# Two graph layers on one core: new places for statistics, weight sums, exponentials and adds in the first and last groups

## The chip, the cores and the metric

The kernel runs on one core of one Trainium2 chip. A core has five engines that run side by side, each with its own queue of instructions: TensorE (PE, with PEld for its weight loads), VectorE (DVE), ScalarE (ACT), GpSimd (POOL) and SyncE (SP). DMA transfers are started from the queues of SP, ACT and POOL. The metric is device time in microseconds (us) of one execution; the kernel before takes 2524.23 us (median of 3 runs, 2522.88 to 2525.54).

## The reference

There are 128 graphs of 128 nodes with 512 features, in fp32, and one 128 x 128 adjacency matrix. Two layers follow each other:

```python
# --- layer 0 ---
h = relu(layernorm(x))
q, k, v = h @ Wq.T, h @ Wk.T, h @ Wv.T
rel = adj.T * (q @ k.T)                    # per graph, 128 x 128
rel = rel / norm(rel, axis=2)
x = x + rel @ v
# --- layer 1 ---
h = relu(layernorm(x))
q, k, v = h @ Wq + bq, h @ Wk + bk, h @ Wv + bv     # 8 heads of 64
scores = q @ k.T / sqrt(64) + where(adj == 0, -1e9, 0)
x = x + softmax(scores) @ v
```

## The kernel before, in words

**Groups.** Four graphs make a group (`G = 4`), so there are 32 groups. A group is a `Layer0` object while it is in layer 0 and a `Layer1` object in layer 1. In the order strings below, `f` is the group that is being fetched and normalized for layer 0, `m` the group whose layer 0 is computed, `n` the same group as it enters layer 1, `l` the group whose layer 1 is computed, `p` the one whose layer 1 is being finished. `w` is an object with the steps that prepare the weights of layer 1.

**Order by hand.** All five engines run under a manual schedule: each engine executes its instructions in the order in which the program emits them. The order strings `FIRST`, `SECOND`, `ORDER` and `LAST` are lists of steps, and `run` calls the step methods from left to right. `FIRST` serves the first group, `SECOND` the second, `ORDER` all others, `LAST` the end. So a step's place in a string fixes its place in every queue that it uses, and an instruction that has to wait holds up everything behind it on its engine. Before `FIRST` there is a prologue: the statistics and transposition of group 0, the first loads, and the weights of layer 0.

**Products.** A 512 x 512 x 512 product is a `Product` object made of seven products of half size (`P1` to `P7`). `wc[n]` holds the weights' quarters and four sums of them, made by `sums` with four adds of 128 x 512: T1, T2, T3, T4N, in this order. `P1`, `P2` and `P3` use plain quarters (W11, W21, W22); `P5`, `P6`, `P7` and `P4` use T1, T2, T3 and T4N. On the other side stand quarters of the transposed activations and the sums `s[0]` to `s[3]`, which `sumA` (s0, s1) and `sumB` (s3, s2) make on DVE. A product keeps its results in three PSUM banks, x, y and z; the pool `ps_mm` has four banks. `P1` starts bank x and ACT copies it out (`r1`); `P2` starts y and DVE adds `r1` to it; `P5` starts z, copied by ACT (`r5`); `P6` goes on in x, copied (`r2`); `P3` goes on in z, and DVE adds `r2`; `P7` goes on in x, and DVE adds `r5`; `P4` goes on in x and ACT copies it. The copies lie in the pool `rpool`, four buffers used in turn. `G`, `V` belong to layer 0; `Q`, `K`, `V` to layer 1 (with biases).

**Other steps.**
- `stat(b)`: two DVE instructions per graph, L283 and L284. `inv(i)`: four small POOL instructions for two graphs, L290 to L293, giving `rstd` and `shift`.
- `hn(i)`: two ACT instructions (L301) normalize two graphs; ACT then sends them to DRAM (`d_h`, L184). `rd(i)`: four DMAs on SP (L192) fetch them in another arrangement (`u_h`). `T(i)`: DVE transposes 32 x 32 blocks (L313) into `h`. In the prologue `hn_pe` and `turn_pe` do the same through TensorE (L335).
- `weights0` multiplies Wq and Wk of layer 0 into one matrix on TensorE (`pa`, L123), DVE copies the four results out (`place`, L114 and L115) and makes the sums of `a`. `weights_v0` transposes Wv on TensorE (`pwv`, L139, PSUM banks of the same pool as `pa`), ACT copies it out, and POOL makes the sums `v0` from the buffer `v12` of `rpool`.
- `load1` issues the weights of layer 1 as DMAs from POOL's queue. `w.scale` is three ACT multiplies on the weights of q; `w.sumq`, `w.sumk` are sums on DVE, `w.sumv` on POOL.
- `R`, `mask_rel`, `square`, `N`, `norms`, `O`, `xO`: layer 0's 128 x 128 products on TensorE (L382), mask on DVE (L391), squares on ACT (L398), their sums on TensorE (L408), the root `rn` on DVE and POOL (L417, L418), the output product (L422), and the residual add on DVE (L428).
- `S`, `mk`, `ex`, `wr`, `wt`, `A`, `oc`, `rdo`, `ot`: layer 1's scores on TensorE (L453, one set of PSUM banks: `S1` waits until `ex0` has read the scores of graph 0), mask and maximum on DVE, exponentials on ACT (L471), their way through DRAM (`d_w`, `u_w`) and DVE's transposition, the output product (L570), its copy by ACT (L581), the way back (`d_o`, `u_o`), the division by the sums on DVE (L598), and POOL's residual add (L605).
- In `LAST` the last two graphs go another way: `mkA`, `mkB`, `exA`, `exB`, `tw` (L519), `An` (L530), and `fin(b)`, which divides on DVE (L539), adds to x on POOL or DVE (L547) and sends the result from SP (L548).

`load(g, b, queue)` starts the load of one graph's x (L70). `xpool` has twelve buffers, so three groups fit. The method `Layer.load` issues one only if the graph isn't loaded or being loaded yet.

Of the kernel before, what the change touches and what calls it, by code (L numbers as in the profile page):

```python
# [11 lines left out]
ALU = mybir.AluOpType  # L12
# [3 lines left out]
G = 4  # L16
# [5 lines left out]
def kernel(  # L22
# [15 lines left out]
    nc = tc.nc  # L38
# [29 lines left out]
    def load(g: int, b: int, queue):  # L68
        xb = xpool.tile([P, D], F32, tag="xb", name=f"xb_{g}_{b}")
        queue.dma_start(xb, x[g * G + b])  # L70
        x_tiles[g, b] = xb
# [16 lines left out]
    def sums(n: str, w12, eng):  # L88
        c = wc[n]
        eng.tensor_tensor(c[:, T1], w12, c[:, W11], ALU.subtract)  # L90
        eng.tensor_tensor(c[:, T2], c[:, W22], c[:, T1], ALU.subtract)
        eng.tensor_tensor(c[:, T3], c[:, W22], w12, ALU.subtract)
        eng.tensor_tensor(c[:, T4N], c[:, W21], c[:, T2], ALU.subtract)
# [16 lines left out]
    w12 = {}  # L110

    def place(n: str, m: int, ps, w12, copy):

        copy(wc[n][:, W11 if m < 2 else W21, m % 2, :], ps[:, 0:HF])  # L114
        copy(w12[:, m, :] if m < 2 else wc[n][:, W22, m % 2, :], ps[:, HF:D])  # L115

    def weights0(between):

        a12 = rpool.tile([P, 2, HF], F32, tag="r", name="a12")
        pa = [ps_mm.tile([P, D], F32, tag="mm", name=f"pa_{m}") for m in range(KD)]  # L120
        for k in range(KD):
            for m in range(KD):
                nc.tensor.matmul(  # L123
                    pa[m], lhsT=raw["q"][:, k, ts(m, P)], rhs=raw["k"][:, k, :],
                    start=(k == 0), stop=(k == KD - 1),
                )
            if k == KD - 2:
                between()
        for m in range(KD):
            place("a", m, pa[m], a12, nc.vector.tensor_copy)  # L130
        sums("a", a12, nc.vector)

    def weights_v0():

        v12 = rpool.tile([P, 2, HF], F32, tag="r", name="v12")
        for m in range(KD):
            pt = ps_mm.tile([P, KD, P], F32, tag="mm", name=f"pwv_{m}")
            for k in range(KD):
                nc.tensor.transpose(pt[:, k, :], raw["v"][:, k, ts(m, P)], ident)  # L139
            place("v0", m, pt.rearrange("p k e -> p (k e)"), v12, nc.scalar.copy)  # L140
        sums("v0", v12, nc.gpsimd)
        nc.vector.tensor_scalar(mask, adj_sb, 0.0, NEG, ALU.is_equal, ALU.mult)

    def load1():
        for name, w in (("q", wq1), ("k", wk1), ("v1", wv1)):
            wr = w.rearrange("(k p) d -> p k d", p=P)
            nc.gpsimd.dma_start(
                wc[name][:, W11 : W21 + 1].rearrange("p h k d -> p (h k) d"), wr[:, :, 0:HF]
            )
            nc.gpsimd.dma_start(wc[name][:, W22], wr[:, 2:4, HF:D])  # L150
            w12[name] = wpool.tile([P, 2, HF], F32, tag="wT", name=f"w12_{name}")
            nc.gpsimd.dma_start(w12[name], wr[:, 0:2, HF:D])
        nc.gpsimd.dma_start(bq_sb, bq1.rearrange("(e p) -> p e", p=P))
        nc.gpsimd.dma_start(bk_sb, bk1.rearrange("(e p) -> p e", p=P))
        nc.gpsimd.dma_start(bv_sb, bv1.partition_broadcast(P))

    class Weights1:
        def scale(self):

            SC = HD**-0.5  # L160
            nc.scalar.mul(wc["q"][:, 0:3], wc["q"][:, 0:3], SC)
            nc.scalar.mul(w12["q"], w12["q"], SC)
            nc.scalar.mul(bq_sb, bq_sb, SC)

        def sumq(self):
            sums("q", w12["q"], nc.vector)
# [199 lines left out]
    class Layer0(Layer):  # L366
        n = 0
# [62 lines left out]
    class Layer1(Layer):  # L430
        n = 1
# [104 lines left out]
        def fin(self, b):  # L536
            g, xb = self.g, x_tiles.pop((self.g, b))
            o = work.tile([P, D], F32, tag="o", name=f"o_{g}_{b}")
            nc.vector.tensor_tensor(  # L539
                o.rearrange("p (k r d) -> p k r d", k=NH, r=2),  # L540
                self.po.pop(b).rearrange("p (k r d) -> p k r d", k=NH, r=2),
                self.rs.pop(b).rearrange("p (r k) -> p k r", r=2)[:, :, :, None].to_broadcast(
                    [P, NH, 2, HD]
                ),
                ALU.mult,
            )
            (nc.vector if b == G - 1 else nc.gpsimd).tensor_tensor(xb, xb, o, ALU.add)  # L547
            nc.sync.dma_start(out[g * G + b], xb)  # L548

        def mkA(self, b):  # L550
# [58 lines left out]


    FIRST = """
        m.sumA m.sumB m.start m.G.P1 f.hn0 f.rd0 m.G.P2 m.G.P5 w.scale m.G.P6 w.sumq m.G.P3 m.V.P1 f.hn1 f.rd1
        w.sumv m.G.P7 m.V.P2 w.sumk m.G.P4 m.V.P5
        m.R m.mask_rel m.square f.T0 m.V.P6 m.V.P3 m.N m.norms m.V.P7 m.O0 m.xO0 m.O1 m.xO1 n.stat0 n.stat1
        n.inv0 m.V.P4 n.hn0 n.rd0 f.T1 m.O2 m.O3 f.sumA f.start f.G.P1 m.xO2 m.xO3 n.stat2 n.stat3 n.inv1
        f.G.P2 f.sumB f.G.P5 n.hn1 n.rd1 f.G.P6 f.G.P3 f.G.P7 n.T0 f.G.P4 n.T1 n.start
    """.split()
    SECOND = """
        l.Q.P1 l.sumA l.Q.P2 l.sumB l.K.P1 l.K.P2 l.Q.P5 l.Q.P6 f.load0 f.load1 l.Q.P3 l.K.P5 l.K.P6 l.Q.P7
# [16 lines left out]
    """.split()  # L636
    LAST = """
        l.Q.P1 p.rdo0 l.sumA l.Q.P2 l.sumB l.K.P1 l.K.P2 p.wt3 l.Q.P5 p.ot0 l.Q.P6 l.Q.P3 l.K.P5 l.K.P6 l.K.P3
        l.Q.P7 l.S0 l.mk0 l.K.P7 l.Q.P4 l.ex0 l.wr0 l.K.P4 l.S1 l.mk1 p.A1 p.oc1 p.rdo1 l.start_v l.V.P1
        l.ex1 l.V.P2 l.V.P5 l.S2 l.mkA2 l.mkB2 l.V.P6 l.exA2 l.exB2 l.wt0 l.wr1 l.V.P3 l.V.P7 l.S3 l.mkA3 l.mkB3  # L640
        l.tw2 l.wt1 l.exA3 l.exB3 l.V.P4 l.An0 l.fin0 l.An1 l.fin1 p.ot1 l.tw3 l.An2 l.fin2 l.An3 l.fin3
    """.split()
# [1 line left out]
    def run(order, **who):  # L644
        for step in order:
            name, *path = step.split(".")
            at = who.get(name)
            if at is None:
                continue
            if len(path) == 2:  # L650
                getattr(getattr(at, path[0]), path[1])()
            elif path[0][-1].isdigit():
                getattr(at, path[0][:-1])(int(path[0][-1]))
            else:
                getattr(at, path[0])()

    with tc.manual_schedule(engines={EN.PE, EN.SP, EN.Pool, EN.DVE, EN.Activation}):
        p, l, m = None, None, Layer0(0)
        for b in range(G):
            m.stat(b)  # L660
        m.inv(0)
        m.inv(1)
        for b in range(G):
            load(1, b, nc.gpsimd)
        load1()
        m.hn_pe(0)
        m.hn_pe(1)
        f = Layer0(1)
        for b in range(G):
            f.stat(b)  # L670
        f.inv(0)
        f.inv(1)
        weights0(lambda: m.turn_pe(0))
        m.turn_pe(1)
        weights_v0()
        for g in range(NG):
            n = Layer1(g)
            if g:
                f = Layer0(g + 1) if g + 1 < NG else None
            run((FIRST, SECOND, ORDER)[min(g, 2)], p=p, l=l, m=m, n=n, f=f, w=Weights1())  # L680
            p, l, m = l, n, f
        run(LAST, p=p, l=l)
# [30 lines left out]
```

## Time and profile before

| | us |
|---|---|
| median of 3 runs | 2524.23 |
| lowest, highest | 2522.88, 2525.54 |
| the profiled execution, its own time | 2526.15 |
| its span in the trace | 2524.4 |
| TensorE busy in the span | 2497.9 (99%) |
| DVE busy | 1709.2 (68%) |
| ACT busy | 1022.3 (40%) |
| POOL busy | 534.7 (21%) |

The profile is of one execution, whose own time is 1.92 us above the median; about 1.75 us of it lie outside the span. A line of the timeline reads: start, length, engine, line of the code, operation, output <- inputs, shapes, and in brackets the idle time of the engine before it with what ended it. "PE" rows of eight matmuls with L218 are one half-size product. POOL's times are rough, and TensorE's ends are modelled.

### The profile page before, as it was taken

What the parts mean: (1) busy time and instruction counts of PE and PEld (TensorE: products, weight loads), DVE (VectorE), ACT (ScalarE), POOL (GpSimd) and SP (SyncE); (2) the same over time, 40 slices, a digit from 0 to 9 for tenths busy, and PEclk for the clock granted to TensorE, in tenths of its full rate; (3) what the DMA queues carried; (4) which work ended last, traced back from release to release, by engine and by line L of the source; (5) the groups of instructions that cost most, each with busy time, mean ns of one, the idle gap of its engine ahead of it and who ended that gap; (6) DMA issues with size and microseconds to landing.
All of it is one profiled execution on the core that took longest, in us unless ns stands there. A gap on an engine that the chain in (4) does not pass through costs nothing.

```text
span 2524.4 us, 40790 instructions
## 1 busy us (share of the span) xinstructions
PE 2497.9 (99%) x14672; PEld 2106.7 (83%) x14672; DVE 1709.2 (68%) x2484; ACT 1022.3 (40%) x3248; POOL 534.7 (21%) x945
## 2 busy tenths in 40 slices
PE   8999999999999999999999999999999999999998
PEld 6788888888888888888888888888888888888886
DVE  5566766676776667666767766676667676666766
ACT  3344443444433444344444434443444444344433
POOL 4121222112122212221121222122211212221211
PEclk9999999999999999999999999999999999999999
DMA  5255554556445555445564455554455644555543
GB/s 172 84 176 175 166 156 141 182 161 199 147 145 159 176 175 167 152 147 176 160 197 146 144 165 173 178 167 152 147 175 162 197 148 143 164 176 176 167 135 101
DMA packets 370475, 405.71 MB, mean 161 GB/s; under 512 B 29600, under 2 KB 286752, under 8 KB 370272
## 3 DMA queue, kind: packets, MB, share of 16 engines
q1 hardware_dynamic: 278992, 167.92, 25.2%
q10 hardware_dynamic: 70384, 166.74, 18.4%
q0 software_dynamic: 20896, 68.44, 8.2%
q8 instruction: 115, 1.88, 0.3%
q14 instruction: 88, 0.72, 0.1%
HBM read 204.80 MB, written 198.18 MB: 160 GB/s over the span
## 4 chain that ended last, share of the span: by engine, by line
PE 97%; DVE 1%; DMA 1%; ACT 0%; issue 0%; POOL 0%; SPq 0%; ACTq 0%; DVEq 0%; POOLq 0%
PE pv_x L218 18%; PE pq_x L218 9%; PE pv_z L218 9%; PE pk_x L218 9%; PE pg_x L218 9%; PE pss L453 6%; PE po L570 5%; PE pv_y L218 5%; PE pg_z L218 4%; PE pq_z L218 4%; PE pr L382 4%; PE pk_z L218 4%; PE po L422 4%; PE pk_y L218 2%; PE pg_y L218 2%; PE pq_y L218 2%
## 5 line engine op out<-in xcount | busy, mean ns | idle before, releaser
L471 ACT ACTIVATE e<-pss,nmax 128x128 f32<-128x128 f32 x1008 | 354.1, 379 | 178.0 <-DVE nmax L464 156.2
L605 POOL TENSOR_TENSOR xb<-xb,o 128x512 f32<-128x512 f32 x124 | 158.3, 1276 | 1108.8 <-DVE o L598 1083.9
L218 PE MATMUL pv_x<-wc_v,h 128*128 128x256 f32 x1280 | 300.8, 382 | 0.0
L218 PEld LDWEIGHTS pv_x<-wc_v,h 128*128 128x128 f32 x1280 | 240.3, 190 | 51.0 <-DVE v L242 11.8
L301 ACT ACTIVATE hn<-xb,shift,rstd 128x512 f32<-128x512 f32 x252 | 190.9, 807 | 153.5 <-POOL shift L293 153.4
L313 DVE STREAM_TRANSPOSE h<-u_h 128x1024 f32<-128x1024 f32 x126 | 156.4, 1242 | 133.0 <-DMA u_h<-d_h 130.4
L218 PE MATMUL pv_z<-wc_v,s 128*128 128x256 f32 x1024 | 246.0, 383 | 0.0
L471 ACT ACTIVATION_READ_ACCUMULATOR e<-pss,nmax 128x1 f32 x1008 | 220.7, 219 | 0.0
L218 PEld LDWEIGHTS pv_z<-wc_v,s 128*128 128x128 f32 x1024 | 192.6, 191 | 29.2 <-DVE pv_r L235 0.4
L462 DVE TENSOR_TENSOR pss<-pss,mask 128x1024 f32<-128x1024 f32 x126 | 154.7, 1228 | 81.0 <-PE pss L453 75.5
L218 PE MATMUL pv_x<-wc_v,s 128*128 128x256 f32 x768 | 184.9, 384 | 0.0
L218 PE MATMUL pq_x<-h,wc_q 128*128 128x256 f32 x768 | 184.8, 383 | 0.0
L283 DVE BATCH_NORM_STATS2 st<-xb 128x6 f32<-128x512 f32 x256 | 172.1, 672 | 16.0 <-DMA xb<-in_x_dram 16.0
L218 PE MATMUL pk_x<-h,wc_k 128*128 128x256 f32 x768 | 181.5, 379 | 0.0
L453 PEld LDWEIGHTS pss<-kT,qT 64*128 64x128 f32 x2048 | 124.2, 187 | 54.4 <-issue 27.0
L218 PEld LDWEIGHTS pq_x<-h,wc_q 128*128 128x128 f32 x768 | 143.2, 190 | 23.8 <-ACT oT L581 5.1
L218 PEld LDWEIGHTS pk_x<-h,wc_k 128*128 128x128 f32 x768 | 145.8, 190 | 19.9
L290 POOL TENSOR_SCALAR rstd<-mv 128x2 f32<-128x2 f32 x128 | 28.9, 226 | 630.0 <-DVE mv L284 629.8
L218 PEld LDWEIGHTS pv_x<-wc_v,s 128*128 128x128 f32 x768 | 140.8, 190 | 20.5 <-issue 0.2
L464 DVE TENSOR_REDUCE nmax<-pss 128x8 f32<-128x1024 f32 x126 | 154.3, 1224 | 4.3
L486 DVE STREAM_TRANSPOSE wT<-u_w 128x1024 f32<-128x1024 f32 x126 | 150.7, 1196 | 5.2 <-DMA u_w<-d_w 5.0
L453 PE MATMUL pss<-kT,qT 64*128 64x128 f32 x2048 | 148.7, 285 | 2.6 <-ACT e L471 2.3
(147 smaller groups left out, 4416.8 us busy)
## 6 DMA issues: line engine op xcount, KB each, us to landing
d_h<-hn ACTq DMA_DIRECT2D x126, 512.0 KB, 3.6
u_h<-d_h SPq DMA_DIRECT2D x504, 128.0 KB, 3.5
d_w<-e ACTq DMA_DIRECT2D x126, 512.0 KB, 2.7
u_w<-d_w SPq DMA_DIRECT2D x504, 128.0 KB, 3.1
xb<-in_x_dram POOLq DMA_DIRECT2D x124, 256.0 KB, 3.3
d_o<-oT ACTq DMA_DIRECT2D x62, 512.0 KB, 4.3
u_o<-d_o SPq DMA_DIRECT2D x248, 128.0 KB, 3.6
out_dram<-xb POOLq DMA_DIRECT2D x124, 256.0 KB, 3.0
```

Of the source, the lines that this page charges most:

```text
L218: nc.tensor.matmul(ps[:, m, :], lhsT=lhsT, rhs=rhs, start=first and m == 0 and k == 0, stop=k == 1, skip_group_check=True,)
L283: nc.vector.bn_stats(st, x_tiles[g, b])
L301: nc.scalar.activation(hn[:, r], x_tiles[g, b].rearrange("p (k j q) -> p j k q", j=TB, q=BK), AF.Relu, bias=self.shift[:, b : b + 1], scal ...
L313: nc.vector.transpose(half.rearrange("p k (t i) -> p t k i", i=BK), self.u.pop(i).rearrange("p t (k q) -> p t k q", q=BK),)
L382: nc.tensor.matmul(pr[:, b, :], lhsT=self.turned(k, b), rhs=self.gT[:, k, ts(b, P)], start=(k == 0), stop=(k == KD - 1),)
L453: nc.tensor.matmul(pss[:, r, k, :], lhsT=self.qT[rows, k, ts(b, P)], rhs=self.kT[rows, k, ts(b, P)], start=True, stop=True,)
L462: nc.vector.tensor_tensor(sc, sc, mask[:, None, :].to_broadcast([P, H, P]), ALU.add)
L464: nc.vector.tensor_reduce(self.nmax[b], sc, AX.X, ALU.max, negate=True)
L471: nc.scalar.activation(e[:, :, i, :], sc[:, i, :].rearrange("p (j q) -> p j q", q=BK), AF.Exp, bias=nmax[:, i : i + 1], accum_out=self.tot ...
L486: nc.vector.transpose(self.wT[b].rearrange("p h (t i) -> p t h i", i=BK), self.uw.pop(b).rearrange("p t (h q) -> p t h q", q=BK),)
L570: nc.tensor.matmul(po[r * HD : (r + 1) * HD, k, :], lhsT=self.v[:, b, ts(2 * k + r, HD)], rhs=wT[:, r * NH + k, :], start=True, stop=True,)
L605: nc.gpsimd.tensor_tensor(xb, xb, o.rearrange("p k t q -> p (k t q)"), ALU.add)
```

## The change

The change alters places only; what is computed stays the same, apart from which engine does one add.

- The statistics of group 1 (`f.stat`, `f.inv`) leave the prologue, where they stood ahead of `weights0`, and go into `FIRST`, two graphs after `m.start` and two after `m.G.P2`.
- The sums of `v0` on POOL leave `weights_v0` and become the step `w.sumw` behind `f.inv1`.
- `f.hn0 f.rd0` move from behind `m.G.P1` to behind `m.G.P5`, `w.scale` from behind `m.G.P5` to behind `m.G.P6`.
- `w.sumq` moves from behind `m.G.P6` to behind `m.V.P2`; `w.sumk` moves from behind `m.V.P2` to the layer 0 products of group 1, behind `f.sumB`.
- A new step `w.loadx` issues the four loads of group 2's x from POOL's queue behind `w.sumv`. In `SECOND` the steps `f.load0` to `f.load3` then find them loaded and issue nothing.
- `m.xO2 m.xO3 n.stat2 n.stat3 n.inv1` move ahead of `f.sumA f.start f.G.P1`.
- In `LAST`, `l.ex0 l.wr0` move ahead of `l.Q.P4`.
- `fin(2)` adds on DVE, as `fin(3)` does, in place of POOL.

```diff
@@ weights_v0
             place("v0", m, pt.rearrange("p k e -> p (k e)"), v12, nc.scalar.copy)
-        sums("v0", v12, nc.gpsimd)
+        w12["v0"] = v12
         nc.vector.tensor_scalar(mask, adj_sb, 0.0, NEG, ALU.is_equal, ALU.mult)
@@ class Weights1
+        def sumw(self):
+            sums("v0", w12["v0"], nc.gpsimd)
+
+        def loadx(self):
+            for b in range(G):
+                load(2, b, nc.gpsimd)
@@ Layer1.fin
-            (nc.vector if b == G - 1 else nc.gpsimd).tensor_tensor(xb, xb, o, ALU.add)
+            (nc.vector if b >= G - 2 else nc.gpsimd).tensor_tensor(xb, xb, o, ALU.add)
@@ orders
     FIRST = """
-        m.sumA m.sumB m.start m.G.P1 f.hn0 f.rd0 m.G.P2 m.G.P5 w.scale m.G.P6 w.sumq m.G.P3 m.V.P1 f.hn1 f.rd1
-        w.sumv m.G.P7 m.V.P2 w.sumk m.G.P4 m.V.P5
+        m.sumA m.sumB m.start f.stat0 f.stat1 f.inv0 m.G.P1 m.G.P2 f.stat2 f.stat3 f.inv1 w.sumw m.G.P5 f.hn0 f.rd0 m.G.P6
+        w.scale m.G.P3 m.V.P1 f.hn1 f.rd1 w.sumv w.loadx m.G.P7 m.V.P2 w.sumq m.G.P4 m.V.P5
         m.R m.mask_rel m.square f.T0 m.V.P6 m.V.P3 m.N m.norms m.V.P7 m.O0 m.xO0 m.O1 m.xO1 n.stat0 n.stat1
-        n.inv0 m.V.P4 n.hn0 n.rd0 f.T1 m.O2 m.O3 f.sumA f.start f.G.P1 m.xO2 m.xO3 n.stat2 n.stat3 n.inv1
-        f.G.P2 f.sumB f.G.P5 n.hn1 n.rd1 f.G.P6 f.G.P3 f.G.P7 n.T0 f.G.P4 n.T1 n.start
+        n.inv0 m.V.P4 n.hn0 n.rd0 f.T1 m.O2 m.xO2 m.O3 m.xO3 n.stat2 n.stat3 n.inv1 f.sumA f.start f.G.P1
+        f.G.P2 f.sumB w.sumk f.G.P5 n.hn1 n.rd1 f.G.P6 f.G.P3 f.G.P7 n.T0 f.G.P4 n.T1 n.start
     """.split()
     LAST = """
         l.Q.P1 p.rdo0 l.sumA l.Q.P2 l.sumB l.K.P1 l.K.P2 p.wt3 l.Q.P5 p.ot0 l.Q.P6 l.Q.P3 l.K.P5 l.K.P6 l.K.P3
-        l.Q.P7 l.S0 l.mk0 l.K.P7 l.Q.P4 l.ex0 l.wr0 l.K.P4 l.S1 l.mk1 p.A1 p.oc1 p.rdo1 l.start_v l.V.P1
+        l.Q.P7 l.S0 l.mk0 l.K.P7 l.ex0 l.wr0 l.Q.P4 l.K.P4 l.S1 l.mk1 p.A1 p.oc1 p.rdo1 l.start_v l.V.P1
@@ prologue
         f = Layer0(1)
-        for b in range(G):
-            f.stat(b)
-        f.inv(0)
-        f.inv(1)
         weights0(lambda: m.turn_pe(0))
```

## The prediction

> **What bounds the kernel now.** The page first: TensorE is busy for 99% of the span, so over the middle of the run nothing can be won by moving work of other engines.
>
> ```profile
> PE 2497.9 (99%) x14672; PEld 2106.7 (83%) x14672; DVE 1709.2 (68%) x2484; ACT 1022.3 (40%) x3248; POOL 534.7 (21%) x945
> ```
>
> So I asked next for TensorE's own waits over the whole run ("waited for: us in total, times, longest"). The four longest beside the first load:
>
> ```profile
> PE pwv L139 <- issue: 3.1, 1, 3.1
> PE pg_x L218 <- DVE gT L242: 2.8, 2, 2.0
> PE pq_z L218 <- DVE qT L242: 2.6, 1, 2.6
> PE pss L453 <- ACT e L471: 2.3, 2, 2.0
> ```
>
> Then the chain of waits shows where they lie and what follows (start, length, what):
>
> ```profile
> 21.54 3.08 issue
> 24.63 3.48 PE pwv L139 x16
> ...
> 42.63 1.29 DVE gT L242 x2
> ...
> 43.96 2.92 PE pg_x L218 x8
> 46.88 2.48 PE pv_z L218 x8
> ...
> 72.18 7.40 DMA d_h<-hn
> ```
>
> Eight matmuls of L218 take 1.73 us elsewhere in this chain, eight transposes of L335 take 0.87. So the work after each of the first two stalls runs at half speed. The stretches give TensorE's granted clock behind the busy times (third number from the end):
>
> ```profile
> 22.00:24.00 2.00, 0.00 (x0) 0.00 (x0) 1.75 (x5) 0.20 (x1) 2.00 (x4) 1.00 0.99 334
> 24.00:26.00 2.00, 1.37 (x7) 1.40 (x8) 2.00 (x7) 0.25 (x1) 1.85 (x3) 0.60 1.00 350
> 46.00:48.00 2.00, 2.00 (x7) 1.55 (x6) 1.54 (x3) 0.58 (x1) 0.00 (x0) 0.50 0.30 77
> 84.00:88.00 4.00, 1.43 (x7) 0.94 (x6) 3.81 (x6) 0.05 (x1) 0.00 (x0) 1.00 0.00 0
> ```
>
> The timeline names what the stalls wait for:
>
> ```profile
> 23.80 0.39 DVE L114 COPY wc_a<-pa 128x256 f32<-128x256 f32 x1
> ...
> 40.95 1.75 DVE L93 TENSOR_TENSOR wc_q<-wc_q 128x512 f32<-128x512 f32 x1
> 42.63 0.68 DVE L242 TENSOR_TENSOR gT<-pg_z,pg_r 128x512 f32<-128x512 f32 x1
> ...
> 70.61 2.26 POOL L70 DMA_DIRECT2D xb<-in_x_dram  x4
> ```
>
> ```profile
> 2482.91 0.84 ACT L229 ACTIVATE qT<-pq_x,bq_sb 128x256 f32<-128x256 f32 x2 [7.36 <-PE pq_x L218]
> ...
> 2516.73 1.95 DVE L547 TENSOR_TENSOR xb<-xb,o 128x512 f32<-128x512 f32 x1
> ```
>
> **The change part by part.** The order of TensorE's own instructions is untouched, so I carry its timeline forward and ask, for each wait, whether the operand is there.
>
> *Statistics of the second group, out of the prologue.* DVE's copies of pa (L114) stand behind four f.stat, which wait for x of group 1 until 22.18; the copies start at 23.80 although pa_0 is complete at about 18.1. The pwv transposes need those PSUM banks. Without the stats the copies go out as pa completes, the last at 21.5; pwv starts at 21.54 without a stall: 3.08. The clock then isn't lost: 16 transposes at the 0.109 of L335 are 1.74 in place of 3.48: 1.74. Together 4.8 us. What the stats cost in their new place: DVE's block from the last pa copy to the end of sumB takes 5.3 (26.51 to 31.83), so it ends at 26.8; two stats (0.82 a pair of instructions) end at 28.5. POOL is tied up by load1's DMAs until 28.36 in both versions, so inv0 starts at 28.6 against 28.43. It took 2.86 here and 1.6 to 2.0 later in the trace; I take the slow row, 31.45. stat2, stat3 lie behind the P2 add and end at 30.8, before POOL wants them.
>
> *hn0 one product later; sums v0 named sumw.* ACT then does r5 (by 29.3), hn0 (31.45 to 33.0), r2 (to 33.65). G.P7 on TensorE, now 1.74+3.08 earlier, accumulates over the bank that r2 reads, at 33.65. That is a dead heat: between 0 and 0.5 lost, I take 0.2. POOL's sumw runs 33.3 to 38.4 (4 x 1.28), in the same place on POOL as before. Its third operation frees v12's buffer at about 37.1, which by the rotation of four may hold up V.P1's r copy on ACT, and behind it hn1 and the P4 copy (39.9 at worst); R needs that at 40.6, so the cover is 0.7.
>
> *sumq behind the V.P2 add.* In the trace four SBUF adds of 1.65 to 1.80 (POOL adds at the same time; 0.68 alone) stand before the P3, P7 and V.P2 adds, and G.P4 waits 2.02 for them. Moved back, P7's add is done 0.9 before G.P4 wants it: 2.02. Again the clock: 2.92+2.48 for G.P4 and V.P5 becomes 3.46: 1.94. Together 4.0 us, R begins at 40.6. sumq itself now runs 38.4 to 45.4 beside sumv, and mask_rel behind it ends at 46.1 instead of about 44.9; square ends at 46.8, TensorE wants it at 47.6 after V.P6 and V.P3. Those two products hide it; without them it would cost about 1.3.
>
> Here a rule speaks against me. The Trainium skill, "TensorE: Matmul & The Clock Gate", section "HAM oscillation — how this bites in real kernels", puts the limit for idle gaps at about 3.4 us; both gaps are shorter, so by it no clock is at stake and the sum is 3.7 us smaller. The granted clock of 0.50 after 2.02 idle says otherwise here, while 2.57 idle at 84.9 kept 1.00. I go by the rows.
>
> *What moves with these steps.* f.rd0 and f.rd1 are eight fetches on SP (36.12 to 45.17 before) that wait for the ACT sends behind hn0 and hn1; SP has nothing else in this phase, the first set goes out at about 36 as before, the second a little earlier, and T0 and T1 want them at 46 and 54: hidden, with 4 us or more of cover. w.scale (1.49+0.62+0.19 on ACT) now follows r2 and holds V.P1's r copy to 36.2, inside the 37.1 named above. sumk (3.2 in its old place at 44.42) is taken out of the stretch ahead of mask_rel, where nobody waited for it, so I count nothing for its going.
>
> *loadx.* Four DMA issues, 2.3 in all on POOL (row above), move from 70.6 to behind sumv, about 45.3 to 47.7, in front of rn (norms), which POOL gets at 48.8: cover 1.1, and if it is gone rn is late by the excess. SP's queue isn't reordered. The second send of n (d_h) then has no 1 MB of loads beside it: the 7.40 becomes about 3.2 (median 2.9 in that stretch, 3.2 over the first 160 us). T1 for n comes 4 us earlier; the stall of 2.57 before pq_z, and 0.2 of refilling after it (1.99 for 1.73), goes: 2.8 us. What is late next there is TensorE itself, with about 1.4 to spare. xO2, xO3 and the stats before sumA put s0 at 59.1 against a need at 59.3; sumk (4 x 0.68) ends as the P3 add becomes possible. Both taken at 0; bounds -0.3 to +0.5.
>
> *LAST, ex0 before Q.P4.* nmax is ready at 2481.8, but ACT waits for pq_x first (7.36). With ex0 first, its 2.90 end at 2484.7; K.P4 ends on TensorE at 2484.6. The stall of 1.99 before S1 becomes 0.15: 1.8 us. The copies of Q.P4 and K.P4 then end at 2486.4, before oc1 and V.P1's bank need them. wr0 brings one ACT send and four SP fetches with it; SP keeps its order (rdo0, wr0, rdo1, wr1), and wt0 wants the data only at about 2498, so the earlier fetch gains nothing and costs nothing. A gain above 2.0 is excluded, since K.P4 itself ends then; below, the bound is 1.0, if mk1 or oc1 come to wait for ACT instead.
>
> *Add of fin2 on DVE.* POOL's last add (1.27) blocks DVE's last add, 1.95 for 0.68. Now DVE adds twice: the first beside POOL's second L605 add, ending 0.55 after it (as L598 does: 1.21 and 1.25) at 2516.5, o at 2517.1, the last add at 2517.8 against 2518.68: 0.9 us. The two bounds: 0.5 and 1.3. The output DMA follows the last add as before.
>
> Sum: 4.8 + 4.0 + 2.8 + 1.8 + 0.9 - 0.2 = 14.1 us. The profiled execution took 2526.15 (span 2524.4 and 1.75 around it), so 2512.05; the median of the runs shown lies 1.92 below that execution, so 2510.1.
>
> **Rivals.** *The third stall stays or another takes its place* (22%): the send's 7.40 is not the loads' doing, or s0, r2 or rn come a little late. For: thin covers of 0.2 to 1.1. Against: typical sends of 2.9. Gain 8 to 11.5, about 2514.5. *The dead heat is lost* (9%): hn0 late on ACT delays r2, G.P7 waits 2 us, and the clock halves again as it did after 2.02 idle: with later waits the gain falls to 5 to 8, about 2518. *Too small to tell, or the order doesn't take effect as read* (3%): within 5.0 us, which is 0.2% and about what a measurement of this kernel can tell from no change. *Slower* (4%): loadx on POOL is blocked ahead of rn, since POOL's queue is in order; then O2 lacks its PSUM bank and TensorE stands. The cover is 1.1 on POOL and about 2 until O2; from a hold of 17 us beyond the issues' 2.3 the gain is gone, and from 22 us the kernel is slower by more than 0.2%. At such a hold of 30 us the time would be about 2537 (30 - 3.1 lost against 14.1). Nothing in the trace shows an issue above 0.8, all twelve buffers of xpool suffice for three groups.
>
> **How the numbers follow.** Forecast 62%, 2508 to 2512.5; rivals 22, 9, 3 and 4%. A range of 2507.5 to 2516 takes in the forecast, the first rival and the bounds above. Faster by over 0.2%: 93%; same 3%; slower 4%.
>
> **What would show it.** pwv at 21.5 with a clock of 1.00 through 20 to 50; G.P4 without a wait, R at about 40.6; d_h of n's second half landing in under 4 us and no wait of pq_z for qT; in LAST, S1 about 0.15 after K.P4; the last DVE add of 0.7. It is wrong if TensorE waits for r2 near 33, N for sq near 47, or if the middle slices fall below their present busy share.

## The result and the profile after

The changed kernel takes 2512.07 us (median of 6 runs, 2511.32 to 2513.92) against 2524.22 in the same group of runs: a ratio of 0.9953, 95% interval 0.9941 to 0.9966. A second group gave 2512.45 and 0.9947 (0.9933 to 0.9960). That is 12 to 13 us faster; 14.1 was forecast.

The profiled execution took 2513.92, its span is 2512.1. Of the four entries that stood at the top of TensorE's own waits before (waited for: total, times, longest), those of pwv and pq_z are gone, the one for gT fell from 2.8 to 0.8 and the one for e from 2.3 to 0.5. What is left at the top:

```profile
PE pa L123 <- DMA raw_q<-in_L_gnn_Wq_dram: 5.1, 1, 5.1
PE pg_x L225 <- DVE gT L249: 0.8, 1, 0.8
PE po L429 <- ACT v L233: 0.7, 1, 0.7
PE pw L526 <- DVE o L546: 0.5, 1, 0.5
PE pss L460 <- ACT e L478: 0.5, 2, 0.3
```

The chain of waits (start, length, what; the code moved down by seven lines, so L218 is L225 now) runs through the three old stalls of the first groups without a gap:

```profile
5.09 13.61 PE pa L123 x24
18.71 0.87 PE pt L342 x8
...
23.02 0.87 PE pt L342 x8
23.89 1.75 PE pwv L139 x16
25.64 1.73 PE pg_x L225 x8
...
37.72 1.73 PE pv_y L225 x8
39.45 1.73 PE pg_x L225 x8
41.18 1.73 PE pv_z L225 x8
42.90 3.57 PE pr L389 x32
...
76.63 1.73 PE pk_y L225 x8
78.36 1.73 PE pq_z L225 x8
```

The work that ran at 0.60 and 0.50 before (pwv, and G.P4 with V.P5) now lies at 23.9 to 25.6 and at 39.5 to 42.9. The granted clock, the third number from the end, is 1.00 in these stretches:

```profile
24.00:26.00 2.00, 2.00 (x18) 1.95 (x17) 1.97 (x4) 2.00 (x8) 2.00 (x3) 1.00 0.91 270
32.00:40.00 8.00, 8.00 (x39) 7.04 (x38) 2.75 (x6) 5.99 (x9) 7.41 (x12) 1.00 0.61 183
40.00:50.00 10.00, 10.00 (x67) 8.97 (x68) 8.30 (x7) 2.39 (x4) 8.07 (x8) 1.00 0.67 204
```

And the end of its chain:

```profile
2470.07 1.94 PE pk_x L225 x8
...
2475.66 1.16 PE pss L460 x16
...
2506.23 0.69 DVE xb L554
```

The two spans differ by 12.3. Cut at the same instructions in both chains, the difference is:

| block, from and to | before | after | gained | forecast |
|---|---|---|---|---|
| first pt to pg_x of G.P1 | 11.76 | 6.93 | 4.83 | 4.8 |
| to R | 21.26 | 17.26 | 4.00 | 4.0 |
| to pq_z of Q.P5 | 38.10 | 35.46 | 2.64 | 2.8 |
| to S0 of LAST | 2390.66 | 2390.62 | 0.04 | 0 |
| S0 to S1 | 8.46 | 6.68 | 1.78 | 1.8 |
| S1 to the end of the last DVE add | 32.09 | 31.26 | 0.83 | 0.9 |
| from there to the end of the span | 5.72 | 5.18 | 0.54 | not counted |
| start to the first pt | 16.35 | 18.71 | -2.36 | 0 |

The middle of the run is the same to 0.04 us in 2390. The blocks with a forecast came out, 14.1 us in sum, the end of the span gave 0.54 more, and 2.36 were lost before the first block, where the change moves nothing of TensorE's: pa's first 24 pieces began 0.8 later and took 13.61 for 12.06. The column "before" is the profile from which the forecast was made, so the agreement shows that nothing new stood in the way afterwards; it doesn't show that these stalls are typical of the kernel before. So the questions for the experiments: is that start chance, and if it is, why do the medians still differ by only 12 to 13?

### The profile page after: what moved, and what is told of

It reads as the page before. It is cut to its first block, busy times and chain, and to the rows that moved or that the text cites. A ratio compares the mean times of both kernels' runs of the same rounds, so it can differ in the third digit from the quotient of the medians.

```text
span 2512.1 us, 40787 instructions
## 1 busy us (share of the span) xinstructions
PE 2495.4 (99%) x14672; PEld 2104.9 (84%) x14672; DVE 1707.6 (68%) x2485; ACT 1023.6 (41%) x3248; POOL 532.3 (21%) x944
## 4 chain that ended last, share of the span: by engine, by line
PE 97%; DVE 1%; DMA 1%; ACT 1%; issue 0%; SPq 0%; POOL 0%; ACTq 0%; DVEq 0%
PE pv_x L225 18%; PE pq_x L225 9%; PE pg_x L225 9%; PE pv_z L225 9%; PE pk_x L225 9%; PE pss L460 5%; PE pg_z L225 5%; PE po L577 5%; PE pv_y L225 4%; PE pq_z L225 4%; PE pr L389 4%; PE pk_z L225 4%; PE po L429 4%; PE pg_y L225 2%; PE pk_y L225 2%; PE pq_y L225 2%
## 5 line engine op out<-in xcount | busy, mean ns | idle before, releaser
L225 PE MATMUL pv_x<-wc_v,h 128*128 128x256 f32 x1280 | 300.8, 382 | 0.0
L225 PEld LDWEIGHTS pv_x<-wc_v,h 128*128 128x128 f32 x1280 | 240.3, 190 | 51.0 <-DVE v L249 11.7
L225 PE MATMUL pv_z<-wc_v,s 128*128 128x256 f32 x1024 | 245.1, 382 | 0.0
L225 PEld LDWEIGHTS pv_z<-wc_v,s 128*128 128x128 f32 x1024 | 192.0, 190 | 28.6
L225 PE MATMUL pv_x<-wc_v,s 128*128 128x256 f32 x768 | 184.9, 384 | 0.0
L225 PE MATMUL pq_x<-h,wc_q 128*128 128x256 f32 x768 | 184.7, 383 | 0.0
L225 PE MATMUL pk_x<-h,wc_k 128*128 128x256 f32 x768 | 181.5, 379 | 0.0
L225 PEld LDWEIGHTS pq_x<-h,wc_q 128*128 128x128 f32 x768 | 143.3, 190 | 23.6 <-ACT oT L588 5.1
L225 PEld LDWEIGHTS pk_x<-h,wc_k 128*128 128x128 f32 x768 | 145.8, 190 | 19.9
L225 PEld LDWEIGHTS pv_x<-wc_v,s 128*128 128x128 f32 x768 | 140.8, 190 | 20.6 <-issue 0.2
```

The source lines that it names most:

```text
L225: nc.tensor.matmul(ps[:, m, :], lhsT=lhsT, rhs=rhs, start=first and m == 0 and k == 0, stop=k == 1, skip_group_check=True,)
```

## The experiments

Each kernel was timed in five rounds or more against the kernel before on the same chip. Three groups ran on three chips; ratios are against before in the same group. The changed kernel ran again in the first group only (with "hn0 behind G.P6", "Products in the first stall" and the first warm start), so "slower" below is the distance from its 2512.45 and in most cases lies between chips. The medians of before in the three groups are 2525.66, 2524.56 and 2524.38, so a distance of about 1 us isn't clear by itself; the blocks of the traces are given beside it.

**The changed kernel again.** No edit.

> The changed kernel as it is, once more, beside the others of this group. The profiled pair gave 14.6 us of gain behind the first TensorE work and 2.4 us of loss inside it (pa's first 24 pieces took 13.6 us for 12.1 and began 0.8 later), yet the timed medians differ by 12.15. Theory 1 (clock): TensorE's half-speed phases fall differently in every execution, both at the start and behind the old stalls, so the profiled 3.7 us of clock is more than the average; another profile of this kernel should show another length of pa's 24 pieces (12 to 14 us) with everything behind it shifted as a block, and R 24.2 us after the end of those pieces' first transposes, within 0.3. Theory 2 (moved wait): in executions with an earlier start the wait of G.P7 for r2 appears, since POOL's statistics hang on load1's DMAs and not on TensorE; then an early start shows a gap before G.P7 of up to 2 us. Median expected within 1.5 us of 2512.

Measured: 2512.45 (2511.83 to 2513.35), ratio 0.9947. Its chain:

```profile
4.83 12.43 PE pa L123 x24
17.26 0.87 PE pt L342 x8
...
34.55 1.73 PE pg_x L225 x8
...
41.46 3.57 PE pr L389 x32
```

R begins 24.20 us after the first pt, against 24.19 in the other profile: everything behind the start moves as one block. G.P7 (pg_x at 34.55) follows without a gap although the start was earlier, so the moved wait was not seen here. The times of this kernel spread by 2.6 us over its 11 executions in both groups, and its clock is 0.999 in all of them. The kernel before is different. Its 47 executions in the three groups, by the mean granted clock of each:

| mean clock | executions | mean us | from, to |
|---|---|---|---|
| 0.996 | 7 | 2527.99 | 2526.61, 2529.47 |
| 0.997 | 13 | 2526.07 | 2524.36, 2527.61 |
| 0.998 | 24 | 2524.29 | 2521.75, 2526.49 |
| 0.999 | 3 | 2522.34 | 2521.53, 2523.75 |

The same program spreads over 8 us, and time goes with clock: 1.9 us for each 0.001. The profiled execution of before is one at 0.997. Its three executions at the clock of the changed kernel, 0.999, still take about 10 us more than the changed kernel does: which suggests (from three executions, and a clock given to 0.001) that some 10 of the 12 to 13 us are waits and the rest goes with the clock.

**hn0 behind G.P6.**

```diff
-  ... w.sumw m.G.P5 f.hn0 f.rd0 m.G.P6
-  w.scale ...
+  ... w.sumw m.G.P5 m.G.P6 f.hn0 f.rd0
+  w.scale ...
```

> The changed kernel with f.hn0 f.rd0 one product later still, behind G.P6, so that ACT copies r2 before it waits for POOL's shift. Theory 2 (G.P7 waits for r2 in typical executions): 1 to 2.4 us faster than the changed kernel, about 2510. Theory 1 (clock): no difference, within 0.7 us of the changed kernel, since G.P7 did not wait in the profiled execution.

Measured: 2512.69 (2512.62 to 2513.97), ratio 0.9948, no difference from the changed kernel beside it on the same chip. The second theory falls as an account of the missing 2 us: r2 doesn't cost them.

**Products in the first stall of before.**

```diff
         m.turn_pe(1)
+        hot = ps_o.tile([P, D], F32, tag="po", name="hot")
+        for i in range(3):
+            nc.tensor.matmul(hot, lhsT=raw["q"][:, 0, 0:P], rhs=raw["k"][:, 0, :], start=True, stop=True)
         weights_v0()
```

> The kernel before with three products of 128x512 put on TensorE into its first stall (behind the second set of transposes, ahead of pwv; their results are not used). The stall stays, pwv still starts at about 24.6, but TensorE is busy in it. Theory 1: the clock is then full at pwv, its 16 transposes take 1.75 us in place of 3.48, and the median falls by 1.7 us times the share of executions in which the clock was halved there: 0.9 to 1.7 us below before. Rival (the slow transposes come from waiting for the banks one by one, not from the clock): pwv still takes 3.5 us and the time stays within 0.5 us of before.

Measured: 2525.34 (2522.88 to 2529.35) against 2525.66, ratio 0.9999 (0.9991 to 1.0007): no gain to be seen, and still a spread of 6.5 us. The interval reaches down to 2.3 us, so the timing alone doesn't exclude the 0.9 to 1.7 of the expectation; the chain and the granted clock behind it show why half of that can't come:

```profile
25.91 0.66 PE pwv L139 x4
26.58 0.66 PE pwv L139 x4
...
44.16 1.99 PE pg_x L218 x8
46.15 1.73 PE pv_z L218 x8
```

```profile
24.00:29.00 5.00, 4.70 (x23) 2.69 (x22) 4.62 (x12) 2.35 (x8) 3.57 (x5) 1.00 1.00 341
```

With the clock at 1.00, each four of the sixteen transposes still take 0.66: that is the pace of two L114/L115 copies of 0.33 that free one bank. Of the 1.74 that the forecast put down to the clock behind the first stall, 0.9 is this pace, and at most 0.8 the clock. (Both went, since in the changed kernel the copies run while pa still computes.) The second stall was 1.7 us long in this execution, and the products behind it ran at full speed; in the profile of before the stall of 2.0 was followed by 2.92 and 2.48. So the same gap doesn't always halve the clock.

**Parts undone, one at a time.** All from the changed kernel.

*Statistics back in the prologue.*

```diff
-  m.start f.stat0 f.stat1 f.inv0 m.G.P1 m.G.P2 f.stat2 f.stat3 f.inv1 w.sumw
+  m.start m.G.P1 m.G.P2 w.sumw
...
+        for b in range(G):
+            f.stat(b)
+        f.inv(0)
+        f.inv(1)
         weights0(lambda: m.turn_pe(0))
```

> The changed kernel with only the statistics of group 1 back in the prologue (all other parts of the change kept). The first stall must come back: DVE's copies of pa start behind the last stat, at about 23.8 to 25, and pwv waits 3 us. By the prediction's term 4.8 us slower than the changed kernel (2517). By what the run with products in the stall showed (banks are freed 0.66 apart, so pwv takes 2.64 even at full clock): 3.1 + 0.9 for sure and up to 0.8 for the clock, so 4.0 to 4.8. Rival (a stall so early is absorbed by the wait of G.P7 for r2, since hn0 hangs on POOL): 2 us or less.

Measured: 2516.27 (2515.08 to 2517.72), ratio 0.9966 (0.9954 to 0.9979); 3.8 slower than 2512.45, just under the expected 4.0 to 4.8. The stall is back in its waits and its chain, with a fallen clock behind it:

```profile
PE pwv L139 <- issue: 2.9, 1, 2.9
```

```profile
24.47 3.52 PE pwv L139 x16
```

```profile
24.00:28.00 4.00, 3.53 (x17) 3.56 (x18) 3.97 (x11) 1.94 (x6) 2.87 (x4) 0.57 1.01 327
```

In this trace the block from the first pt to G.P1 takes 11.64 (16.34 to 27.98) against 6.93: 4.7, the size of the term. The start of this execution was as quick as that of before.

*hn0 back behind G.P1.*

```diff
-  m.G.P1 m.G.P2 f.stat2 f.stat3 f.inv1 w.sumw m.G.P5 f.hn0 f.rd0 m.G.P6
+  m.G.P1 f.hn0 f.rd0 m.G.P2 f.stat2 f.stat3 f.inv1 w.sumw m.G.P5 m.G.P6
```

> The changed kernel with f.hn0 f.rd0 back behind G.P1, ahead of r5 on ACT. ACT then holds r5 until POOL's shift (about 31 to 33) and two normalizations are through, r5 ends about 33.5 to 35.5, and G.P3, which wants it at about 30.5 to 31.5, waits 3 to 4 us; with that a chance of a halved clock behind it. Expected 3 to 5.5 us slower than the changed kernel, with a wider spread of its runs. Rival (hn0's place is free, what matters are the stats alone): within 0.7 us.

Measured: 2517.06 (2515.13 to 2518.25), ratio 0.9968 (0.9956 to 0.9980); 4.6 slower, inside the expected 3 to 5.5, and with a spread of 3.1. The wait has its name, and the clock behind it (third from the end) fell:

```profile
PE pg_z L225 <- ACT pg_r L233: 4.0, 1, 4.0
```

```profile
34.00:40.00 6.00, 5.29 (x17) 4.38 (x18) 0.69 (x1) 3.07 (x5) 5.91 (x5) 0.72 0.54 176
```

From the first pt to R it takes 30.18 (16.84 to 47.02) against 24.19: 6.0 in this execution, the slowest of its six. So the move of hn0 behind P5 carries as much as that of the statistics: without it the wait goes from pwv to r5.

*sumq back ahead of P3's add.*

```diff
-  w.scale m.G.P3 ... m.V.P2 w.sumq m.G.P4
+  w.scale w.sumq m.G.P3 ... m.V.P2 m.G.P4
```

> The changed kernel with w.sumq back ahead of G.P3's add. The prediction's term: 2.0 of wait and 1.9 of clock, 4.0 slower (2516). The run with products in the first stall showed the same wait of 1.7 with full clock behind it. Theory (the clock falls only in some executions): 2.0 to 3.5 slower in the median, and a wider spread than the changed kernel's 1.5 us, with granted clocks of 0.998 among the runs. Rival (sumq's four adds end before they hurt, since POOL's sums are later now): under 1 us.

Measured: 2520.10 (2518.68 to 2522.56, 16 runs), ratio 0.9982 (0.9974 to 0.9989); 7.6 slower, more than twice the 2.0 to 3.5 that were expected. Its waits, and DVE in its timeline:

```profile
PE pg_x L225 <- DVE gT L249: 5.4, 2, 4.6
```

```profile
36.47 0.73 DVE L90 TENSOR_TENSOR wc_q<-w_q,wc_q 128x512 f32<-128x512 f32 x1 [4.07 <-ACT w_q L162]
...
40.48 1.75 DVE L93 TENSOR_TENSOR wc_q<-wc_q 128x512 f32<-128x512 f32 x1
42.15 0.68 DVE L249 TENSOR_TENSOR gT<-pg_z,pg_r 128x512 f32<-128x512 f32 x1
```

The sums can't begin before w.scale on ACT (36.47, before it was 35.85), while TensorE now comes to G.P4 about 3 us sooner; so the wait is 4.6 and no longer 2.0. Behind it G.P4 and V.P5 took 3.78 and 2.16 for 1.73 each, at a granted clock of 0.58: another 2.5, and 7.1 together. The parts aren't independent: each one removes a stall behind which the next one would grow.

*The loads of x back in SECOND.*

```diff
-  f.hn1 f.rd1 w.sumv w.loadx m.G.P7
+  f.hn1 f.rd1 w.sumv m.G.P7
```

> The changed kernel without w.loadx: the four loads of group 2's x go out in SECOND again, behind n.inv1. Prediction's term: d_h of n's second half lands after about 7 us in place of 3, pq_z waits 2.6 for qT, 2.8 slower (about 2515.2). Rival (the send is slow for itself, or T1 came late because of where the statistics stood): d_h lands in about 3, less than 0.8 slower. With a halved clock in some executions up to 1.7 more.

Measured: 2513.86 (2513.15 to 2514.94), ratio 0.9956 (0.9944 to 0.9969); 1.4 slower, half of the term and between the two expectations; by itself it is hardly clear of the distance between chips. The chain shows the mechanism as forecast, with a shorter wait (pk_y ends at 76.63 here, so 1.4 for 2.57):

```profile
63.83 6.43 DMA d_h<-hn
...
78.04 1.99 PE pq_z L225 x8
```

The send d_h is 512 KB. With the 1 MB of loads beside it, it landed in 7.40, 6.8 (in "Products in the first stall") and 6.43 us; in the eleven profiles of kernels that keep w.loadx, no send of this stretch took more than 3.3. So the rival, that the send is slow for itself, falls.

In this profile the dead heat at G.P7 was lost: its start was the earliest of those with the moved statistics (first pt at 16.66), r2 is copied to 33.95, TensorE goes on at 34.00, the product takes 1.99 in place of 1.73, and R begins 24.51 after the first pt instead of 24.20. That is the moved wait of the second theory, at 0.3 us and not 2.

*ex0 back behind Q.P4.*

```diff
-  l.K.P7 l.ex0 l.wr0 l.Q.P4 l.K.P4
+  l.K.P7 l.Q.P4 l.ex0 l.wr0 l.K.P4
```

> The changed kernel with l.ex0 l.wr0 behind l.Q.P4 again. Prediction's term: S1 waits 2.0 for the exponentials in place of 0.2, everything behind it is later by as much: 1.8 slower (about 2514.2), in some executions up to 1.7 more if the clock falls behind the wait. Rival (the end hangs on the last DVE and DMA work and has slack): under 0.6.

Measured: 2515.14 (2513.94 to 2515.71), ratio 0.9960 (0.9946 to 0.9973); 2.7 slower, inside the expected 1.8 to 3.5. The wait is there again:

```profile
PE pss L460 <- ACT e L478: 2.3, 2, 2.0
```

From S0 to S1 its chain takes 8.47 against 6.68: 1.8, the size of the term. The clock stayed at 1.00 behind it in this profile; that the rest of the 2.7 is clock in other executions is possible (two of its five runs have 0.998), but not shown. The move of fin2's add was not run by itself; its 0.83 is read from the two chains. The moves of w.sumw, w.scale, w.sumk and of xO2, xO3 with their statistics were not undone either; nothing was counted for them.

**Towards a faster version.** The start was the largest loss left, so TensorE was kept busy before its weights land. This version and the three behind it also have hn0 behind G.P6, as above.

```diff
+    hot = ps_o.tile([P, P], F32, tag="po", name="hot")
+    for i in range(8):
+        nc.tensor.matmul(hot, lhsT=ident, rhs=ident, start=True, stop=True)
...
-            if k == KD - 2:
+            if k == KD - 1:
                 between()
```

> The changed kernel with hn0 behind G.P6 as in e9, with eight products of 128x128 on TensorE from about 1.3 us on, before the first weights land (results not used), and with the first transposes of h behind all of pa. Theory 1: the clock is full sooner, pa's 24 pieces take 10.3 to 11.5 us in place of 12 to 13.6, the spread of the runs shrinks, and the median falls 1 to 3 us below the changed kernel (2509 to 2511). Rival (the slow beginning of pa is a wait for the weights' loads): pa takes as long as before, no gain; up to 0.5 us slower by the products that are added.

Measured: 2518.31 (2515.09 to 2519.39), ratio 0.9967, 5.9 slower than the changed kernel on the same chip. Outside the hand-made order the products came out behind ten pieces of pa (at 11.44 in the chain), so this run says nothing on the idea. In its trace R began at 43.95, and TensorE waited 2.1 for the squares (sq) at N of the second group. With the same lines as the first ones inside the manual schedule:

> As the run with products ahead of the first weights, but now they stand first in TensorE's order (there they came out behind ten pieces of pa, and cost time without warming anything): eight products of 128x128 from 1.4 us on; hn0 behind G.P6; the first transposes behind all of pa. Theory 1: the clock is full about 3 us sooner against pa; pa's 32 pieces take 14 to 15.5 us in place of 16 to 17, transposes in a row cost 0.6 of waiting, net 0.5 to 2 us faster than the changed kernel. Rival (the first pieces are slow because their weights land late): no gain, 0 to 1 us slower.

Measured: 2513.52 (2511.99 to 2515.35), ratio 0.9955 (0.9943 to 0.9968): no gain. Yet pa's 32 pieces took 14.37 in one go for 15.87 and 17.05 (24 and 8 together) in the two profiles of the changed kernel, and R began at 40.77. In the profiled execution, the slowest of the five (2515.35), the gain was lost later, at N of the second group:

```profile
5.13 14.37 PE pa L123 x32
...
98.49 4.86 DMA d_w<-e
...
111.95 3.54 PE pv_x L225 x8
```

The send of the weights took 4.86 where 2.6 to 2.8 is usual, DVE's mask stands behind that data, N waited 1.8 for it, and the product behind took 3.54 for 1.92, at a granted clock of 0.58. So there was an edit for this, and another for the 0.8 that G.P4 waits for P7's add:

```diff
-  f.G.P7 n.T0 f.G.P4 n.T1 n.start
+  f.G.P7 n.T0 n.T1 n.start
...
-  l.Q.P1 l.sumA ...
+  l.Q.P1 m.G.P4 l.sumA ...
...
-  l.wr1 l.wt0 m.R m.mask_rel m.square
+  l.wr1 m.R m.mask_rel l.wt0 m.square
```

> A version that should beat both: the changed kernel with hn0 behind G.P6; with group 1's G.P4 taken out of FIRST and put behind l.Q.P1 in SECOND, so that a product lies between P7 and P4 (P4 waits 0.8 for DVE's add of P7 in all traces so far); and with SECOND's m.mask_rel ahead of l.wt0, so that the mask doesn't stand behind the data from DRAM on DVE (that wait cost 1.8 us and a halved clock in two of the profiles). Theory: 1.0 to 1.5 us faster than the changed kernel (2511), with no wait for sq at about 110. Rival (the waits are met again one step later, by wt0 or by pq's banks): within 0.5 of the changed kernel.

Measured: 2514.52 (2513.54 to 2515.08), ratio 0.9958: 2 slower than the changed kernel, and outside both expectations, though the rival's reason (the wait is met again one step later) holds. Q.P1 needs T0, and T0 stands on DVE behind P7's add, which in turn waits for P7:

```profile
PE pq_x L225 <- issue: 2.0, 1, 2.0
```

```profile
69.18 2.82 PE pq_x L225 x8
72.00 2.56 PE pg_x L225 x8
```

The wait of 0.8 became 2.0, and the two products behind it took 2.82 and 2.56 for 1.73, at a granted clock of 0.57. The wait for sq is gone from its list, so the other edit did its part. Last, this version with the eight products first in TensorE's order and the transposes behind all of pa:

> The version before this one in the list, with the eight products on TensorE ahead of the first weights and the first transposes behind all of pa. In the run that had the warm start alone R began 0.7 to 2.1 us earlier than in three profiles of the kernel without it (40.8 against 41.5, 41.7 and 42.9), and the gain was lost to the wait for sq at 110. If that wait is what ate it, this version is 0.7 to 2 us faster than the other (2509 to 2510); if the early start is taken back elsewhere (r2, sumq ahead of mask_rel), no difference.

Measured: 2513.53 (2512.56 to 2514.75), ratio 0.9955: 1.0 below the run before it, at the low end of the expectation but with overlapping runs (2513.54 to 2515.08 there), and not below the changed kernel. No version of these beats the changed kernel.

## Why the prediction was right, and where its sizes were off

**Right.** The direction, the range, and the mechanism of the parts: in the table above every block came out within 0.2 of its term, and each of the four stalls came back when its part was undone (fin2's add alone was not undone). The covers held and were wider than forecast in the profile after: POOL was free 2.9 before rn (forecast 1.1), the squares were done 2.1 before N (0.8). The hold of V.P1's copy by v12 didn't show: in the second profile the copy began at 35.55, while POOL's third operation ran to 37.00. The debit of 0.2 for r2 was 0 in two profiles of the changed kernel and 0.3 in the run without loadx; in the first two a late start hid it, which is luck. Going by the rows for the clock was right too. The rule of about 3.4 us, which the prediction takes from the Trainium skill ("TensorE: Matmul & The Clock Gate", "HAM oscillation — how this bites in real kernels"), would have left no clock to win. But shorter gaps were followed by a low granted clock in further runs: 2.9 by 0.57 (statistics back), 2.0 by 0.57 and 1.8 by 0.58 (two of the versions that were meant to be faster). The gaps of 4.0 and 4.6 fit the rule. Other short gaps kept 1.00: 1.7 (products in the stall) and 2.0 (ex0 back). So no length of gap divides the two here.

**Too large.** The sum was 14.1, the medians moved by 12.15 and 13.2; the intervals of the two ratios (8.6 to 14.9 us and 10.1 to 16.9) both hold 14.1, so this shortfall alone isn't clear of noise. The forecast median of 2510.1 was clearly too low, though: the lowest of the 11 executions of the changed kernel is 2511.32. The step that failed is the one that took one profiled execution as the measure of each term and then took off 1.92 more ("the median of the runs shown lies 1.92 below that execution, so 2510.1"). That execution had a long third stall, a clock of 0.997 and a quick start. By the table of clocks, 1.92 is what one step of 0.001 costs, so it is likely (an estimate, not shown) that the 1.92 was clock which the 14.1 had taken off already: without it the forecast is 2512.05, beside 2512.07 measured. That the two agree so closely is luck, since the start differs too. Term by term:
- *The stall before pq_z, 2.8:* 1.4 when the loads alone were put back; 1.5 in another profile of the old order, and 2.57 in the one that was read. It hangs on the landing of one send (7.40, 6.8 and 6.43 in these), so its length isn't fixed, and the one that was read was the longest of the three.
- *The clock behind the first stall, 1.74:* 0.9 of it is the pace at which the banks come free. The amount was right, its cause only in part.
- *The statistics, 4.8:* 3.8 in the medians when they were put back, 4.7 in the block of that trace; so the term isn't shown to be too large.
- *The clock in general:* by the table, before loses 0.0015 of mean clock against the changed kernel's 0.999, at 1.9 us per 0.001 some 2.8 us, which is about the 3.7 less that 0.9. So the clock term was about right on average.
- *The start:* first pt at 16.35 in the profile of before; 17.26 and 18.71 in the two of the changed kernel, 16.34 to 18.58 in the others that keep this start. It differs between executions of one kernel, and the old profile had drawn a low one. The three profiles with the statistics in the prologue have 16.34, 16.35 and 17.36, the eight without them 16.66 to 18.71; that the change delays the start by up to 1 us is a rival that these few profiles don't exclude.

These leave up to about 1 us open: undone parts don't add up (they overlap), and a profile of each timed run wasn't taken.

**Rivals.** That the third stall stays or another takes its place: it went in all profiles that keep loadx, and the 12 to 13 us lie above that rival's 8 to 11.5. The lost dead heat cost 0.3 once and not 2. The block of POOL by loadx didn't occur: 2.26 for its four issues, and rn came without delay.

## What to carry to other kernels

Where the busiest engine is at 99%, list its own waits and cut the two chains at the same instructions: each stall's worth in these two executions can then be read to 0.2 us. A stall on TensorE costs its length and, in these profiles, between nothing and 2.5 us more through the clock behind it, and both differ from one execution to the next; take the mean of several profiles before adding them up. If a profiled execution is slower than the median because of the stalls that the change removes, don't take that difference off a second time. When a step is moved to free one engine, look at once at what stands behind it in its new queue: statistics moved without hn0, or hn0 without sumq, would have handed the wait on.

## What the runs showed of the hardware

The same binary of before took 2521.5 to 2529.5 us, in step with its mean granted clock, while the changed kernel with its gaps closed stayed within 2511.3 to 2513.9. Gaps of 2.0 us were followed by a clock of 0.50 in one execution and 1.00 in another. A send of 512 KB to DRAM landed in 6.4 to 7.4 us with 1 MB of loads beside it and in at most 3.3 without. At the start, TensorE ran at half pace for 3.1 us in one profile and 6.1 in another (pieces 0.86 apart in place of 0.43), though the granted clock is shown as 1.00 there: the pace of the pieces tells it, the column doesn't. The weight loads of pa show where the pace changes, first in the profile before, then in the one after:

```profile
7.01 0.34 PEld L123 LDWEIGHTS pa<-raw_k,raw_q 128*128 128x128 f32 x1 [0.52 <-issue]
7.60 0.19 PEld L123 LDWEIGHTS pa<-raw_k,raw_q 128*128 128x128 f32 x1 [0.25 <-issue]
8.03 0.19 PEld L123 LDWEIGHTS pa<-raw_k,raw_q 128*128 128x128 f32 x1 [0.24 <-issue]
```

```profile
10.38 0.34 PEld L123 LDWEIGHTS pa<-raw_k,raw_q 128*128 128x128 f32 x1 [0.52 <-issue]
11.23 0.21 PEld L123 LDWEIGHTS pa<-raw_k,raw_q 128*128 128x128 f32 x1 [0.52 <-issue]
11.68 0.19 PEld L123 LDWEIGHTS pa<-raw_k,raw_q 128*128 128x128 f32 x1 [0.24 <-issue]
```
